# Bias of v folded into the projection bias: its columns written by GpSimd at attention's beginning, the product copied by ScalarE and added by GpSimd

## The chip, the cores and the metric

The kernel runs on one core of one Trainium2 chip, as one program in one launch. The metric is the device time of one execution in microseconds (us). Three timed runs of the kernel before gave 1572.09, 1574.92 and 1575.85 us; the median is 1574.92 us.

The engines are named as the profile names them: PE (TensorE matmul), PEld (TensorE weight load), DVE (VectorE), ACT (ScalarE), POOL (GpSimd) and SP (SyncE, which here only issues DMAs). Each runs its own queue in order and waits on semaphores.

## The reference

One transformer block with binarized attention weights and a ternary MLP, in float32. `x` is 4 x 1024 x 256, there are 16 heads of 16 columns.

```python
x = x + layernorm(attention(layernorm(x)))
x = x + layernorm(mlp(layernorm(x)))

def binlinear(x, W, b):                 # alpha: one number per row of W
    return x @ (alpha(W) * sign(W)).T + b
# attention
q, k, v = (split_heads(binlinear(x, W, b)) for W, b in ((Wq, bq), (Wk, bk), (Wv, bv)))
y = softmax(q @ k.T * scale) @ v
return binlinear(merge_heads(y), Wp, bp)
# mlp: tlin(x, w, s) = (x @ w.T) * s, w in {-1, 0, 1}
h = silu(tlin(x, w1, s1)) * tlin(x, w2, s2)
h = gelu(tlin(h, h1, sh1)); h = gelu(tlin(h, h2, sh2))
return tlin(h, w3, s3)
```

Rows of the softmax sum to one, so `bv` passes through attention unchanged. The kernel therefore leaves `bv` out of v and adds `(bv @ sign(Wp).T) * alpha_p` to `bp` once. Only that small piece is changed here: a 256-vector, held as the same row on all 128 partitions.

## The kernel before, in words

**Stages.** A short opening loads x and the weights, takes their signs and magnitudes, and normalises the first half of batch 0. `attention(True)` follows, a schedule that is written out by hand: the order in the source is the order in each engine's queue. Then the MLP runs over eight blocks of 512 tokens.

**Attention.** A block is 512 queries of one batch and four heads; there are 32. Each is worked in eight steps. A step has a first pass (L717: scores with queries on partitions, then a maximum on DVE, L726) for the block that comes next, and a second pass (L763: scores with keys on partitions, minus the maximum; the exponential on ACT, L773) with the product with v (L789) for the current block. Steps -10 to -1 hold only first passes of block 0 and 1 and the work that has to be done once: the projections of q, k and v of batch 0 (L561 for the first four heads, L530 for the others, L489 for v), the alphas (`alphas`, L992 and L999), and `projection_bias` at step -2. At the beginning of step -2 the maxima of block 0 are combined (`combine`: L733 on DVE, L735 to L737 on POOL), and in step -1 they are turned by PE (`shift`, L743) and copied by ACT (L750, `nmT`). The second pass of block 0 starts at step 0 with that copy.

**PSUM banks.** `through` is seven banks of 128 x 512. `bank()` gives out the bank that a small cost model (`clock`, `free_at`) holds to be free first; `put` and `got` keep that model and state the dependences, so the choice of the bank, made when the program is built, decides which reader a matmul waits for.

**The piece in question.** `projection_bias` first makes `bv_cols` on DVE (L396: each value of `bv` repeated along a row of 128), PE multiplies it with the signs of `Wp` (L401, two matmuls over one bank), DVE multiplies the bank by `az_bc`, the alphas of `Wp` (L406), and DVE adds that to `bz_bc` (L407). `bz_bc` is read for the first time when the first half of batch 0 is projected (L647), long after. `bv_cols` is a tile of the tag `full`, which has two buffers and also carries the pieces of q and k on their way from ACT (L537) to POOL (L543, L544). From those, SP copies the heads of the second four into place with 24 DMAs (L600).

**GpSimd's beginning.** On entering attention POOL clears `negmax` (L347), sets the ones in v's tiles (L431, L432) and clears `yn` (L436) and `bits` (L898), while DVE normalises the second half of batch 0 (L460, `xn`) and PE and ACT make the first heads' q (L561, L567). Later POOL also gathers the low bits of the MLP's weights (`gather`, L921 to L924) through a tile `half` of 128 x 512.

Of the kernel before, what the change touches and what calls it, by code (L numbers as in the profile page):

```python
# [30 lines left out]
F32 = mybir.dt.float32  # L31
# [4 lines left out]
ALU = mybir.AluOpType  # L36
# [4 lines left out]
P = 128  # L41
# [5 lines left out]
def sandwich_kernel(  # L47
# [24 lines left out]
    nc = tc.nc  # L72
    B, T, C = x.shape
    F = w1T.shape[1]
    KC = C // P
# [24 lines left out]
    ident = const.tile([P, P], F32, tag="ident", name="ident")  # L100
# [22 lines left out]
    bz_bc = const.tile([P, C], F32, tag="bz", name="bz_bc")  # L123
    az_bc = const.tile([P, C], F32, tag="az", name="az_bc")
# [16 lines left out]
    bv_sb = small.tile([P, KC], F32, tag="bv", name="bv_sb", bufs=1)  # L141
# [148 lines left out]
    def attention(signs):  # L290


        with ExitStack() as actx:
            ac = actx.enter_context(tc.tile_pool(name="ac", bufs=1))
# [5 lines left out]
            through = ps.tile([P, 7, 512], F32, tag="through", name="through")  # L300
# [4 lines left out]
            def bank():  # L305
                b = min(free_at, key=free_at.get)
                clock["PE"] = max(clock["PE"], free_at.pop(b))
                return b

            def state(access, engine, after, others, operands=()):  # L310
                for other in others:
                    tc.declare_no_dep(
                        access.ins, group=other, keep=[*after, *operands], reason="another bank"
                    )
                for earlier in after:
                    tc.add_manual_dep(access.ins, earlier.name, SYNC, reason="the same bank")
                tc.add_to_no_dep_group(engine, access.ins)
                return access.ins

            def put(b, access, operands=()):  # L320


                state(access, "PE", read[b], ("ACT", "DVE"), operands)
                if read[b]:
                    written[b].clear()
                    read[b] = []
                written[b].append(access.ins)
                clock["PE"] += 115

            def got(banks, engine, access, for_pe=False):  # L330

                others = [o for o in ("PE", "ACT", "DVE") if o != engine and not (for_pe and o == "PE")]
                after = [i for b in banks for i in written[b] + read[b]]
                lasts = {"ACT": 500, "DVE": 580}[engine]
                clock[engine] = max(clock["PE"] + 240, clock[engine] + lasts)
                for b in banks:
                    read[b].append(access.ins)
                    free_at[b] = clock[engine] + lasts + 150  # L340
                return state(access, engine, after, others)
# [7 lines left out]
            a2 = actx.enter_context(tc.tile_pool(name="a2", bufs=2))  # L349
# [23 lines left out]
            if signs:  # L373
                w_in = sign_of

                low = ac.tile([P, KC, T], F32R, tag="xnT", name="xnT_low")
                xnT_of = [[xnT_sb, low if b > 0 else w1_sb] for b in range(B)]
            else:
                w_in = {n: ac.tile([P, KC, C], F32, tag=f"w{n}", name=f"w{n}") for n in "qkv"}
# [10 lines left out]
                nc.vector.memset(alpha_sb, 1.0)  # L390
                nc.vector.memset(alpha_sb[:, 0, :], SCALE)

            def projection_bias():

                bv_cols = a2.tile([P, 2, KC, P], F32, tag="full", name="bv_cols")
                nc.vector.tensor_copy(  # L396
                    bv_cols[:, 0], bv_sb.unsqueeze(2).to_broadcast([P, KC, P])
                )
                t = bank()
                for i in range(KC):  # L400
                    put(t, nc.tensor.matmul(  # L401
                        through[:, t, :C], bv_cols[:, 0, i, :], w_in["p"].bitcast(F32)[:, i, :],
                        start=(i == 0), stop=(i == KC - 1),
                    ))
                product = bv_cols[:, 1].rearrange("p k o -> p (k o)")
                got([t], "DVE", nc.vector.tensor_mul(product, through[:, t, :C], az_bc))  # L406
                nc.vector.tensor_add(bz_bc, bz_bc, product)  # L407

            def load_scales():
                for dst, src in ((s1_sb, s1), (s2_sb, s2), (sh1_sb, sh1), (sh2_sb, sh2)):  # L410
# [486 lines left out]
            bits = ac.tile([P, 512], F32, tag="bits", name="bits")  # L897
            nc.gpsimd.memset(bits, 0)  # L898

            def weight_jobs():  # L900
                loads, stay, pass_by = [], [], []
                for dst, src in ((w1_sb, w1T), (h1a_sb, h1T[0 : F // 2, :]), (w2_sb, w2T)):
                    sv = src.rearrange("(k p) o -> p k o", p=P)
                    for k in range(0, sv.shape[1], 2):
                        loads.append(
                            lambda to=dst[:, k : k + 2, :], frm=sv[:, k : k + 2, :]:
                            nc.gpsimd.dma_start(to, frm)
                        )
                    for k in range(sv.shape[1]):
                        stay += [dst[:, k, bass.ts(j, 512)] for j in range(F // 512)]  # L910
                for src in (h1T[F // 2 : F, :], h2T, w3T):
                    sv = src.rearrange("(k p) o -> p k o", p=P)
                    width = min(512, sv.shape[2])
                    n = 512 // width
                    for k in range(0, sv.shape[1], n):
                        pass_by += [
                            sv[:, k : k + n, bass.ts(j, width)] for j in range(sv.shape[2] // width)
                        ]

                def gather(w):  # L920
                    low = w.bitcast(U16).rearrange("p (c half) -> p c half", half=2)[:, :, 0]  # L921
                    half = ac.tile([P, 512], F32, tag="half", name="half")
                    nc.gpsimd.tensor_copy(half, low)
                    nc.gpsimd.tensor_add(bits, bits, half)  # L924

                def load(i):
                    if i < len(pass_by):
                        raw_of[i] = a2.tile([P, 512], F32, tag="wraw", name=f"wraw_{i}")
                        nc.sync.dma_start(
                            raw_of[i].rearrange("p (k o) -> p k o", o=pass_by[i].shape[2]), pass_by[i]  # L930
                        )

                def take(i):
                    gather(raw_of.pop(i))
                    load(i + 2)

                some = small.tile([P, 1], F32, tag="some", name="some", bufs=1)

                def any_bits():

                    nc.vector.tensor_reduce(some, bits, AX.X, ALU.max)
                    nc.vector.tensor_scalar(some, some, 0.0, None, ALU.is_gt)

                def decide():

                    t = bank()
                    fl = through[0:1, t, 0:1]
                    put(t, nc.tensor.matmul(fl, some, row_ones, start=True, stop=True))
                    got([t], "DVE", nc.vector.tensor_copy(flag_sb, fl))

                *stay, last = [[lambda w=w: gather(w) for w in stay[i : i + 4]]
                               for i in range(0, len(stay), 4)]
                passing = [lambda i=i: take(i) for i in range(len(pass_by))]
                return loads, sum(stay, []) + [lambda: (load(0), load(1))] + passing, (
                    last + [any_bits, decide]
                )
# [76 lines left out]
            for m in range(NT // 2):  # L1033
                place((after + m, 0), lambda m=m: value(m))
            place((first + 8, 0), projection_bias)
            place((4, 0), load_scales)

# [389 lines left out]
    with tc.If(large < 1) as small_ones:  # L1427
        attention(True)
        few = nc.values_load(flag_sb)
        with tc.If(few < 1) as every_one:  # L1430
            mlp("", False, wp_sb)
        with every_one.Else():
            mlp("L", True, wp_sb)
    with small_ones.Else():
        attention(False)
        mlp("G", True, wp_all)
# [46 lines left out]
```

## Time and profile before

The profiled execution has a span of 1570.2 us; its own time is 1571.97 us, so 1.77 us lie around the span. It is 2.95 us below the median of the timed runs.

| view of the profile | what | us |
|---|---|---|
| busy over the span | PE 97%, DVE 68%, ACT 53%, POOL 28% | 1570.2 |
| timeline | opening, up to the first matmul of attention (L561) | 16.99 |
| timeline | first passes alone, up to the first L763 | 57.55 |
| chain of waits | attention's last product with v ends, the MLP's first matmul starts | 906.16 |
| groups | L726 DVE maximum of 128x512 | 0.680 each |
| groups | L646 and L647 POOL, two inputs, 128x256 | 0.733 and 0.736 each |
| tile `bv_cols` | DVE copy L396, multiply L406, add L407 | 0.294, 0.425, 0.425 |

A row of the timeline gives start and duration, engine, line, operation and output<-input; in brackets stands how long the engine sat idle before and what released it. A row of the chain of waits is a piece of work that the end depended on, in order of time. A row of the table by stretches gives, for each engine, its busy time in the stretch and in brackets the number of instructions (PE, PEld, DVE, ACT, POOL), then the clock that TensorE was granted as a share of full speed, the busy share of the DMA engines and GB/s.

### The profile page before, as it was taken

The numbers are of one execution on the slowest core, as the hardware profiler recorded it, in microseconds if no ns is written. First come the engines' busy times: TensorE is split into PE (matmuls) and PEld (weight loads), VectorE is DVE, ScalarE is ACT, GpSimd is POOL, SyncE is SP. The second block draws the span as 40 slices with busy tenths as digits, with TensorE's granted clock in tenths as the row PEclk, the third lists the DMA queues.
The fourth block names the chain that finished last, engine by engine and source line by source line (L and its number), as shares of the span: only waits on it lengthen the run. The fifth ranks groups of instructions, "written<-read, shape, count | busy, mean of one in ns | idle before, by whom it ended". The sixth has DMA issues, their size and how long they took to land.

```text
span 1570.2 us, 31816 instructions
## 1 busy us (share of the span) xinstructions
PE 1530.7 (97%) x12988; PEld 980.1 (62%) x12988; DVE 1075.3 (68%) x1960; ACT 829.2 (53%) x1495; POOL 437.6 (28%) x592
## 2 busy tenths in 40 slices
PE   7999999999999999999999999999999999999997
PEld 5544445444444444444444477888888888888886
DVE  7779887889887898878899554554545445444443
ACT  4477777777776777777777841413232313232321
POOL 2123133565333662414612150120202020202011
PEclk9799999999999999999999999999999999999999
DMA  1311521132133033211312040000000000000000
GB/s 58 72 19 34 152 47 22 30 75 60 47 79 61 13 70 76 61 29 35 76 36 71 8 138 0 1 14 1 14 1 14 1 14 1 14 1 14 1 14 16
DMA packets 35084, 58.55 MB, mean 37 GB/s; under 512 B 9968, under 2 KB 21488, under 8 KB 34928
## 3 DMA queue, kind: packets, MB, share of 16 engines
q1 hardware_dynamic: 29904, 43.70, 13.0%
q0 software_dynamic: 3792, 11.54, 2.4%
q8 instruction: 104, 1.70, 0.4%
q10 hardware_dynamic: 1232, 1.18, 0.2%
q14 instruction: 52, 0.43, 0.1%
HBM read 24.40 MB, written 4.19 MB: 18 GB/s over the span
## 4 chain that ended last, share of the span: by engine, by line
PE 83%; DVE 9%; ACT 4%; SPq 1%; issue 1%; POOL 1%; DMA 1%; POOLq 0%; DVEq 0%; ACTq 0%
PE g L1214 30%; PE y L789 14%; PE through L763 12%; PE through L717 9%; PE p L1214 7%; DVE nm L726 5%; PE fzp L1328 4%; PE through L530 2%; ACT e L773 2%; SPq L600 1%; PE through L743 1%; PE through L489 1%; PE through L632 1%; ACT ys L804 1%; DVE yt L830 1%
## 5 line engine op out<-in xcount | busy, mean ns | idle before, releaser
L726 DVE TENSOR_REDUCE nm<-through 128x1 f32<-128x512 f32 x1024 | 643.2, 680 | 113.7 <-PE through L717 58.0
L773 ACT ACTIVATE e<-through 128x512 f32<-128x512 f32 x1024 | 545.5, 603 | 161.9 <-PE through L763 145.6
L717 PE MATMUL through<-ks,qs 32*128 32x512 f32 x2048 | 462.5, 446 | 3.7 <-DVE nm L726 1.8
L763 PE MATMUL through<-qs,ks 32*128 32x512 f32 x2048 | 442.8, 435 | 11.2 <-ACT e L773 7.3
L763 PE MATMUL through<-nmT,ones_r 32*128 32x512 f32 x1024 | 349.3, 451 | 0.4 <-ACT nmT L750 0.4
L789 PE MATMUL y<-e,v 128*32 128x256 f32 x4096 | 322.2, 392 | 0.0
L717 PEld LDWEIGHTS through<-ks,qs 32*128 32x128 f32 x2048 | 216.0, 185 | 106.7 <-issue 83.8
L1214 PE MATMUL g<-g,h_sb 128*128 128x512 f32 x1024 | 235.7, 390 | 0.0
L763 PEld LDWEIGHTS through<-qs,ks 32*128 32x128 f32 x2048 | 202.6, 184 | 44.5 <-ACT e L773 20.8
L1214 PEld LDWEIGHTS g<-g,h_sb 128*128 128x128 f32 x1024 | 191.7, 188 | 39.5
L763 PEld LDWEIGHTS through<-nmT,ones_r 32*128 32x128 f32 x1024 | 137.9, 183 | 91.4 <-issue 88.3
L789 PEld LDWEIGHTS y<-e,v 128*32 128x32 f32 x4096 | 86.3, 108 | 170.8 <-issue 150.8
L1257 ACT ACTIVATE g2f<-g,sh_sb 128x512 f32<-128x512 f32 x64 | 44.1, 689 | 200.4 <-PE g L1214 177.4
L1257 ACT ACTIVATE g1f<-g,sh_sb 128x512 f32<-128x512 f32 x64 | 44.1, 690 | 169.7 <-PE g L1214 169.7
L164 POOL TENSOR_SCALAR ve_fz<-mvp_fz 128x4 f32<-128x4 f32 (+1 forms) x8 | 1.9, 234 | 470.7 <-DVE mvp_fz L176 470.7
L1214 PE MATMUL g<-h,h1b_sb 128*128 128x512 f32 x512 | 126.4, 389 | 0.0
L1214 PE MATMUL g<-h,h1a_sb 128*128 128x512 f32 x512 | 126.4, 389 | 0.0
L1184 DVE CAST g<-g2f 128x512 fp32r<-128x512 f32 x64 | 27.8, 434 | 142.0 <-ACT g2f L1257 142.0
L1214 PE MATMUL p<-xnT_sb,w_sb 128*128 128x512 f32 x512 | 117.7, 390 | 0.0
L1214 PEld LDWEIGHTS g<-h,h1b_sb 128*128 128x128 f32 x512 | 96.1, 188 | 19.9
L1214 PEld LDWEIGHTS g<-h,h1a_sb 128*128 128x128 f32 x512 | 96.1, 188 | 19.9
L1214 PEld LDWEIGHTS p<-xnT_sb,w_sb 128*128 128x128 f32 x512 | 95.6, 188 | 19.9 <-issue 0.4
(197 smaller groups left out, 1512.8 us busy)
## 6 DMA issues: line engine op xcount, KB each, us to landing
qs<-h1b_sb SPq DMA_DIRECT2D x240, 64.0 KB, 2.4
ks<-h1b_sb SPq DMA_DIRECT2D x120, 64.0 KB, 2.4
wraw<-in_dram SPq DMA_DIRECT2D x28, 256.0 KB, 2.7
h_sb<-in_dram POOLq DMA_DIRECT2D x4, 1024.0 KB, 8.2
yT<-yt SPq DMA_DIRECT2D x112, 32.0 KB, 2.0
out_dram<-x_sb SPq DMA_DIRECT2D x7, 512.0 KB, 2.8
x_sb<-in_dram SPq DMA_DIRECT2D x3, 1024.0 KB, 6.3
w_sb<-in_dram POOLq DMA_DIRECT2D x3, 1024.0 KB, 8.9
```

The costliest lines, as they stand in the source:

```text
L489: put(t, nc.tensor.matmul(through[:, t, bass.ts(i, C)], xnT_of[b][j][:, k, bass.ts(2 * m + i, P)], w_in["v"][:, k, :], start=(k == 0 and j ...
L530: put(t, nc.tensor.matmul(through[:, t, :], w_in[tag][:, k, bass.ts(c, P)], xnT_of[b][i][:, k, bass.ts(j, 512)], start=(k == 0 and i == 0) ...
L600: queue.dma_start(dst[to, :].bitcast(F32), src[rows, :].bitcast(F32))
L717: put(t, nc.tensor.matmul(through[:, t, :], q_of[u][n][rows, bass.ts(qt, P)], k_of[u][rows, bass.ts(j, 512)], start=(n == 0), stop=(n == 1),))
L726: got([t], "DVE", nc.vector.tensor_reduce(nm_of[blk][:, n4, j, g : g + 1], through[:, t, :], AX.X, ALU.max, negate=True))
L763: t, nc.tensor.matmul(through[:, t, :], lhs, rhs, start=(n == 0), stop=(n == 2)),
L773: exps.append(got([t], "ACT", nc.scalar.activation(e_of[s, g], through[:, t, :], AF.Exp)))
L789: nc.tensor.matmul(y_of[blk][32 * g : 32 * g + 32, cols], v_sb[n // 2][:, n % 2, :, :].rearrange("p h d -> p (h d)")[:, bass.ds((4 * g4 + ...
L1184: nc.vector.tensor_copy(hi, full)
L1214: nc.tensor.matmul(out[c], wk, src[j][:, k, :], start=(k == 0 and i == 0 and j == 0), stop=(k == n_k - 1 and i == len(ws) - 1 and j == 1),)
L1257: nc.scalar.activation(g, ps, AF.Gelu, scale=scale[:, c : c + 1])
L1328: nc.tensor.matmul(out_ps[i][:, :C], g2[j][:, k, bass.ts(i, P)], wk, start=(k == 0 and n == 0 and j == 0), stop=(k == NF - 1 and n == len( ...
```

## The change

The columns of `bv` are made once at the beginning of attention, on POOL instead of DVE, into a tile `spare` that stays: for each of the two columns, `ident * 0 + bv` over 128 x 128. In `projection_bias` the DVE copy is gone, ACT copies the product out of PSUM, and POOL multiplies it by `az_bc` and adds it to `bz_bc`. `gather` uses `spare` in place of `half`, which no longer exists; `bv_cols` no longer takes a turn in the tag `full`. The bank's reader is now stated to be ACT, so the cost model gives out the next banks in another order.

```diff
+            spare = ac.tile([P, 512], F32, tag="spare", name="spare")
+            bv_cols = spare[:, 0:C].rearrange("p (k o) -> p k o", k=KC)
+            for i in range(KC):
+                nc.gpsimd.tensor_scalar(
+                    bv_cols[:, i, :], ident, 0.0, bv_sb[:, i : i + 1], ALU.mult, ALU.add
+                )
+
             def projection_bias():
 
-                bv_cols = a2.tile([P, 2, KC, P], F32, tag="full", name="bv_cols")
-                nc.vector.tensor_copy(
-                    bv_cols[:, 0], bv_sb.unsqueeze(2).to_broadcast([P, KC, P])
-                )
                 t = bank()
                 for i in range(KC):
                     put(t, nc.tensor.matmul(
-                        through[:, t, :C], bv_cols[:, 0, i, :], w_in["p"].bitcast(F32)[:, i, :],
+                        through[:, t, :C], bv_cols[:, i, :], w_in["p"].bitcast(F32)[:, i, :],
                         start=(i == 0), stop=(i == KC - 1),
                     ))
-                product = bv_cols[:, 1].rearrange("p k o -> p (k o)")
-                got([t], "DVE", nc.vector.tensor_mul(product, through[:, t, :C], az_bc))
-                nc.vector.tensor_add(bz_bc, bz_bc, product)
+                product = spare[:, C : 2 * C]
+                got([t], "ACT", nc.scalar.copy(product, through[:, t, :C]))
+                nc.gpsimd.tensor_mul(product, product, az_bc)
+                nc.gpsimd.tensor_add(bz_bc, bz_bc, product)
...
                 def gather(w):
                     low = w.bitcast(U16).rearrange("p (c half) -> p c half", half=2)[:, :, 0]
-                    half = ac.tile([P, 512], F32, tag="half", name="half")
-                    nc.gpsimd.tensor_copy(half, low)
-                    nc.gpsimd.tensor_add(bits, bits, half)
+                    nc.gpsimd.tensor_copy(spare, low)
+                    nc.gpsimd.tensor_add(bits, bits, spare)
```

## The prediction, as put on record before the change was run

> **What bounds the kernel now.** I read the page first, then the chain of waits around the change, then the waits of that stretch, the table by stretches for the clock, and last the timeline of the opening, where two instructions are added.
>
> ```profile
> PE 1530.7 (97%) x12988; PEld 980.1 (62%) x12988; DVE 1075.3 (68%) x1960; ACT 829.2 (53%) x1495; POOL 437.6 (28%) x592
> PEclk9799999999999999999999999999999999999999
> ```
>
> PE carries the whole span, so only a place where PE stands still or runs slowly can give time back. The clock row has its one dent after the first slice in the second, 39 to 79 us, and `projection_bias` lies there. The chain of waits:
>
> ```profile
> 46.21 2.48 DVE nm L726 x4
> ...
> 48.72 0.06 DVE nmfull L733
> 48.79 0.04 issue
> 48.83 0.30 DVE bv_cols L396
> ...
> 49.18 2.07 PE through L401 x4
> 51.25 1.15 PE through L717 x4
> 52.40 2.00 PE through L530 x4
> 54.40 1.15 PE through L717 x3
> 55.55 1.05 PE through L743 x4
> ```
>
> The chain leaves PE at 46.21: DVE first works off four maxima, then the combination, then makes the columns, and only then can L401 start. The waits say the same:
>
> ```profile
> PE through L401 <- DVE bv_cols L396: 2.5, 1, 2.5
> ACT full_False L537 <- PE through L530: 10.4, 2, 8.6
> ```
>
> ACT meanwhile idles for up to 8.6 us. What follows the stall runs at half clock:
>
> ```profile
> 45.00:48.50 3.50, 1.70 (x11) 0.70 (x9) 3.21 (x6) 0.37 (x1) 1.70 (x2) 1.00 0.00 0
> 48.50:55.40 6.90, 6.22 (x16) 3.32 (x16) 2.97 (x8) 0.78 (x1) 0.64 (x4) 0.50 0.00 0
> 55.40:58.80 3.40, 3.40 (x22) 2.46 (x22) 2.07 (x4) 0.59 (x1) 1.84 (x2) 0.50 0.34 60
> 58.80:62.20 3.40, 3.27 (x29) 2.05 (x26) 3.40 (x7) 2.88 (x6) 0.00 (x0) 1.00 0.44 77
> 62.20:69.00 6.80, 6.80 (x53) 3.01 (x53) 4.07 (x7) 3.14 (x6) 0.00 (x0) 0.50 0.59 103
> ```
>
> The clock is 1.00 in the stretch with the stall, 0.50 for 10.2 us after it, 1.00 again, then 0.50 a second time. In rows of 1 us its steps lie at about 48.5, 58.8, 62.2 and 69.0, always about 3.4 us apart or a multiple of it, as if it were set anew every 3.4 us by the stretch before. From 69 us to the MLP it stays at 1.00.
>
> **The change part by part.** Times count from the span's start of the execution of before.
>
> *The stall.* The columns are ready at about 19 us, so L401 waits for nothing on DVE but its bank, whose last maximum ended at 44.7. PE's L717 group in front starts at 45.44; such a group at 40.27 takes 0.68, here its last pair also waits for ACT's az_bc, done at 45.92. I let L401 start at 46.5 instead of 49.18: -2.7.
>
> *The clock behind it.* With no gap I expect 1.00 to hold up to the end of L743. At full clock the same work costs: L401 1.06 (L999, same form, four records in 1.06 on the chain), L717 0.66 (43.79), L530 1.12 (42.66), L717 0.66, L743 0.57 (at 81.41: 0.65 with its tail), together 4.07, so L743 ends at 50.57. Before it took 49.18 to 56.60, 7.42. That is -3.35. Ends: 0 if the clock falls all the same, -3.35 if it holds; I take the latter, since 38.3 to 41.7, with the same sort of work, held 1.00.
>
> The Trainium skill (TensorE: Matmul & The Clock Gate, Part 1: The HAM clock gate) says that the half clock comes after at least one idle window of about 3.4 us, free-running. By that rule a gap of 2.5 us need not have cost the clock and the sum would hold the 2.7 alone; the row 49 to 58 at 0.50 disagrees, so I go by the row.
>
> *What PE meets on the way.* The order of the built program shows the same sequence on PE, with five PSUM groups that follow another reader and from there on the same pattern in other banks. Group by group: L717 behind L401 reuses its bank and waits for ACT's new copy, 47.56 + 0.1 + 0.37 (L1003, same form) = 48.03, while PE comes there at 48.2; L530 and the next L717 wait for maxima that ended at 46.8 and 47.4; L743 waits for POOL's negmax, 49.63, and PE comes at 50.0. Nothing binds, but cover is 0.2 to 0.4 us. Three more semaphore waits in front of L401: under 0.1.
>
> *DVE.* L396, L406, L407 (0.29 + 0.42 + 0.42) and the 2.16 between them go. The next maximum starts at about 48.85 instead of 52.44; the four of block 1 that were done when the second pass began are done by 51.3 again. No further gain, it is the same chain.
>
> *ACT's copy*, 0.37, falls into its idle 8.6: 0. Behind it stands full_False at 49.4.
>
> *POOL's product and sum*, 0.73 + 0.74 (L646, L647) = 1.47, stand behind negmax (49.63) and ahead of the last piece of k (L543, L544), which was ready at 50.2 and now starts at 51.1. SP's 24 DMAs of heads wait for it: first issue at 51.75 instead of 56.00, last one 14.2 later at 66.0 instead of 70.18, landed (0.6 to issue, 2.3 in flight) at 68.9. Their first readers, first passes of the second four heads, stand six steps after the second pass starts: 77.0 before, 71.0 now. Cover falls from 3.9 to 2.1 us; 0, and beyond 8 us of gain the DMAs would be what is late next. SP's queue behind them (x of batch 1, the scales) moves up too.
>
> *The second stretch at half clock.* Steps 0 and 1 have no product with v; DVE works its maxima without a break there, and 3.4 us of it dropped the clock. That stays, shifted along: 0. Ends: -3.0 if it does not come (57.4 to 69.86 is 12.5; 2.4 steps of 2.5 and 3.3 make 9.3), +1.7 if one more 3.4 us falls to half.
>
> *The columns on POOL.* Two instructions of 128 x 128, each between 0.24 (L200 copies, start to start) and 0.61 (half of L460 on POOL, 128x256, 1.22), on an engine that then idles 15 us. What they can hurt is DVE beside them:
>
> ```profile
> 17.08 0.53 POOL L347 MEMSET negmax<- 128x512 f32 x1
> 17.25 2.89 DVE L460 TENSOR_SCALAR xn<-x_sb,mvp_x,rsp_x 128x256 f32<-128x256 f32 x4 [0.40 <-POOL rsp_x L166]
> 18.50 0.53 POOL L898 MEMSET bits<- 128x512 f32 x1
> 19.20 0.78 ACT L567 ACTIVATE qs<-through,bias,alpha 128x512 fp32r<-128x512 f32 x1 [2.88 <-DVE xn L460]
> ```
>
> The first of the four takes 1.92, the others 0.40: it comes through only as POOL's memsets end. Ends: +1.2, if it now also waits for both columns, and 0. I take 0, by the nearest rows with a POOL that reads: at 983.8 and 984.6 a DVE scale took 0.83 instead of 0.41, so it waited for one POOL addition and went ahead of the next; at 10.59 four xn ran at 0.40 beside POOL copies. An xn that comes earlier gains nothing: PE gives ACT the next bank only at 20.7. `spare` for `half` in 44 gathers: the same two POOL instructions, 0.
>
> **Sum:** -2.7 - 3.35 = -6.0, so 1571.97 becomes 1566.0. The median of the runs is 2.95 above that execution: 1574.92 - 6.0 = 1568.9. PE is busy or held by its own pace from there to the end, so I let the gain reach the end whole. What this kernel's times can tell from no change is about 0.3%, 4.7 us.
>
> **The rivals.**
>
> *xn held by the columns* (0.18). The chain from 17.25 on runs through xn, ACT and L561 at 24.47, so +1.15 there is +1.15 at the end: 1570.1. If PE's gap before 24.5 costs another 3.4 us at half clock, +1.7 more: 1571.8. For it: all of POOL's eleven instructions in a row went ahead of xn. Against: those were memsets, the columns read.
> The Trainium skill (SBUF — State Buffer, Who interferes with whom) states this as a rule: POOL and a DVE instruction in a two-port mode lock each other out for a whole instruction, by order of issue. The 1.92 agrees; whether the lock passes over between two reading POOL instructions is what differs.
>
> *The clock falls anyway* (0.12). The new stretch still has many matmuls over 32 rows. Then the stall alone: 1574.92 - 2.7 = 1572.2.
>
> *The second half-clock stretch goes too* (0.06): up to 3.0 more, limited by the DMAs above to about 2.1: 1566.8.
>
> *Slower* (0.07). One mechanism: xn held at the opening, with PE losing 3.4 us stretches at half clock for it (1.7 each). At 1.22 per column, the whole of L460's row, +2.45 and two stretches make +5.85, which only cancels the gain: 1574.8. It decides from a delay of 2.6 us with two stretches on; slower by 0.3% needs over 7 us and two. Nothing in the profile shows such a hold; the chance is for what I don't see.
>
> **How the numbers follow.** The forecast has 0.57 and a range of its own from 1567 to 1570.5, by the spread of the runs shown (1.9) and where the 3.4 us happen to fall. Faster by over 0.3% (below 1570.2): 0.9 of it, the case with more gain, and 0.45 of the held xn: 0.51 + 0.06 + 0.08 and a little of the clock case = 0.66. Slower by 0.3%: 0.05 of the last rival's 0.07. The rest, 0.29, is within. The range reaches from the case with more gain less the spread, 1565.2, to the clock case plus some of it, 1573.0.
>
> **What would show it.** Right: no wait of PE above 0.3 us in front of L401 or the group behind it; L401's records at 0.3 us instead of 0.63; clock 1.00 from 28 us to at least 52; L743 near 50.6 and the first L763 near 51.4 instead of 57.55; xn's first instruction at most 1.9 us. Wrong: xn above 2.5 us; clock 0.50 at 49 to 52; PE waiting for ACT's new copy, or first passes of the second four heads waiting for DMAs near 71 us.

## The result, and the profile after

The changed kernel takes 1566.16 us (median of 6 runs, 1562.58 to 1568.80), against 1574.93 us for the kernel before beside it (6 runs, 1572.09 to 1576.95). The ratio is 0.9945, with a 95% interval of 0.993 to 0.9959. The forecast was 1568.9 us, with a range from 1565.2 to 1573.0 and 0.66 for faster by over 0.3%.

The profiled execution has a span of 1561.5 us and took 1563.28 us. Two rows of its page, busy time and the granted clock:

```profile
PE 1524.4 (98%) x12988; PEld 977.1 (63%) x12988; DVE 1074.3 (69%) x1957; ACT 829.6 (53%) x1496; POOL 439.5 (28%) x596
PEclk9999999999999999999999999999999999999999
```

The dent of the second slice is gone. The chain of waits through the same place:

```profile
45.49 1.19 PE through L722 x8
46.68 1.06 PE through L405 x4
47.74 0.95 PE through L722 x5
48.69 1.12 PE through L535 x4
49.81 0.66 PE through L722 x3
50.47 0.59 PE through L748 x4
51.06 0.71 PE through L722 x5
51.77 4.28 DVE nm L731 x7
```

The chain now stays on PE. DVE's four maxima, the combination and the columns no longer stand in it; the bias matmuls (L405, before L401) start at 46.68 instead of 49.18 and take 1.06 instead of 2.07. The turning of the maxima (L748, before L743) ends at 51.06 instead of 56.60. In the waits of this stretch the new parts on ACT and POOL stand in two rows:

```profile
PEld through L748 <- POOL spare L411: 0.4, 1, 0.4
PEld through L722 <- ACT spare L410: 0.2, 1, 0.2
```

PE no longer waits ahead of L405. The first row is no new cost: where POOL has no such instruction (e_cols below), the same weight load waits the same 0.4 us behind POOL's `negmax`. The one new hold on PE's path is the second row: the scores behind the bias reuse its bank and wait 0.2 us for ACT's copy, so that group takes 0.95 us instead of 0.66. The table by stretches, for the clock (the number behind the five engines' busy times):

```profile
45.00:48.50 3.50, 3.50 (x20) 1.84 (x18) 3.20 (x6) 0.74 (x2) 1.68 (x2) 1.00 0.00 0
48.50:55.40 6.90, 6.79 (x50) 3.94 (x49) 6.47 (x13) 3.54 (x6) 3.84 (x7) 1.00 0.13 23
62.20:69.00 6.80, 6.80 (x96) 3.16 (x92) 6.02 (x11) 4.88 (x10) 0.00 (x0) 1.00 0.48 83
```

Both stretches that ran at 0.50 before now run at 1.00: the one behind the stall, which the forecast counted on, and the second one at 62 us, which it took as staying. The second one is why this execution gains more than forecast. The MLP's first matmul starts at 897.22 instead of 906.09, 8.87 us earlier, and the span is 8.7 us shorter. In the opening, the columns:

```profile
17.63 0.53 POOL L347 MEMSET negmax<- 128x512 f32 x1
17.80 3.00 DVE L465 TENSOR_SCALAR xn<-x_sb,mvp_x,rsp_x 128x256 f32<-128x256 f32 x4 [0.41 <-POOL rsp_x L166]
18.15 0.77 POOL L397 TENSOR_SCALAR spare<-ident,bv_sb 128x128 f32<-128x128 f32 x2
19.74 0.78 ACT L572 ACTIVATE qs<-through,bias,alpha 128x512 fp32r<-128x512 f32 x1 [2.88 <-PE through L566]
```

The four `xn` take 3.00 us in all, against 2.89 before. The first two run beside the columns (0.385 each) and take 0.51 and 0.46 us; it is now the third, from 18.61 us on, that takes 1.87.

Does the larger gain belong to the change, or to where this execution's half-clock stretches fell? The runs below are read with one table. It cuts each profiled execution at three points that the chain and the timeline give: attention's first matmul, the bias matmuls' start, the end of the turning of the maxima, and the MLP's first matmul. The last column lists the half-clock stretches, in units of 3.4 us, with their start.

| execution | opening to bias, us | bias to end of turning | from there to the MLP | at half clock |
|---|---|---|---|---|
| before | 32.19 | 7.42 | 849.5 | 24.7 (1), 48.6 (3), 62.2 (2) |
| after | 29.14 | 4.38 | 846.2 | 26.2 (1) |
| after_again | 33.39 | 4.38 | 846.3 | 30.3 (3) |
| after_third | 33.62 | 4.39 | 849.0 | 25.9 (4), 60.0 (2) |
| e_cols | 29.30 | 4.10 | 849.4 | 25.5 (1), 56.2 (2) |
| e_product | 35.94 | 7.08 | 849.5 | 29.8 (3), 53.7 (5) |
| e_fill_before | 35.70 | 4.17 | 848.5 | 30.5 (3) |
| e_cols_act | 33.40 | 4.39 | 849.2 | 30.1 (3), 518 (1), 737 (1) |
| e_pool_late | 33.39 | 4.38 | 849.3 | 30.0 (3), 518 (1), 737 (1) |
| e_fill_steps | 33.36 | 4.39 | 850.6 | 30.1 (3) |
| e_fill_open | 29.15 | 4.39 | 849.3 | 513 (1), 732 (1) |
| e_fill_open_again | 29.17 | 4.39 | 848.1 | 513 (1) |
| e_fill_open_last | 37.91 | 4.37 | 848.8 | 24.1 (6), 522 (1) |

### The profile page after: what moved, and what is told of

Read it like the earlier page. It is cut to its first block, busy times and chain, and to the rows that moved or that the text cites. A ratio compares the mean times of both kernels' runs of the same rounds, so it can differ in the third digit from the quotient of the medians.

```text
span 1561.5 us, 31820 instructions
## 1 busy us (share of the span) xinstructions
PE 1524.4 (98%) x12988; PEld 977.1 (63%) x12988; DVE 1074.3 (69%) x1957; ACT 829.6 (53%) x1496; POOL 439.5 (28%) x596
## 4 chain that ended last, share of the span: by engine, by line
PE 84%; DVE 9%; ACT 4%; issue 1%; POOL 1%; DMA 0%; SPq 0%; DVEq 0%; ACTq 0%; POOLq 0%
PE g L1218 30%; PE y L794 14%; PE through L768 12%; PE through L722 10%; PE p L1218 7%; DVE nm L731 6%; PE fzp L1332 4%; PE through L535 2%; ACT e L778 2%; PE through L494 1%; PE through L748 1%; PE through L637 1%; ACT ys L809 1%; DVE bnstp_x L175 1%; DVE yt L835 1%
## 5 line engine op out<-in xcount | busy, mean ns | idle before, releaser
L768 PE MATMUL through<-qs,ks 32*128 32x512 f32 x2048 | 441.8, 433 | 11.3 <-ACT e L778 7.3
L768 PE MATMUL through<-nmT,ones_r 32*128 32x512 f32 x1024 | 348.2, 449 | 0.4 <-ACT nmT L755 0.4
L768 PEld LDWEIGHTS through<-qs,ks 32*128 32x128 f32 x2048 | 201.4, 183 | 45.0 <-ACT e L778 20.5
L768 PEld LDWEIGHTS through<-nmT,ones_r 32*128 32x128 f32 x1024 | 137.3, 182 | 90.9 <-issue 87.9
```

The source lines that it names most:

```text
L768: t, nc.tensor.matmul(through[:, t, :], lhs, rhs, start=(n == 0), stop=(n == 2)),
```

## Experiments

**The changed kernel again.** The kernel is unchanged; it ran twice more, each time beside other variants.

> The changed kernel once more, unaltered, for a second profiled execution and more times. Theory (the extra 2.7 us beyond the forecast are the second half-clock stretch, which comes in some executions and not in others): 1562 to 1569 us, with the granted clock of an execution falling as its time rises, and this profile either like the first (no half clock after 30 us) or some 3 us longer with half clock somewhere between 52 and 66 us. Rival (the second stretch is gone for good and the scatter has another source): no half clock after 30 us in any profile, and time and clock not tied together.

> The changed kernel again, beside the one with the filled opening on the same chip. Median 1566 to 1568 us, and in the profiled execution a half-clock stretch of one or three quanta of 3.4 us that begins between 26 and 31 us.

The first gave 1567.54 us (12 runs, 1563.12 to 1571.43; ratio 0.996, 0.9946 to 0.9974), the second 1567.50 us (5 runs, 1564.70 to 1569.95; ratio 0.9954, 0.994 to 0.9967). The table by stretches of the first one:

```profile
26.80:30.20 3.40, 2.54 (x10) 1.42 (x11) 2.48 (x5) 2.41 (x4) 0.00 (x0) 1.00 0.00 0
30.20:40.50 10.30, 10.30 (x42) 7.05 (x42) 6.57 (x12) 1.95 (x3) 1.88 (x2) 0.51 0.01 2
```

and of the second:

```profile
26.00:39.60 13.60, 13.60 (x52) 8.25 (x45) 7.62 (x13) 4.82 (x7) 1.89 (x2) 0.50 0.00 1
60.20:66.90 6.70, 6.70 (x53) 2.87 (x53) 3.95 (x7) 3.07 (x6) 0.00 (x0) 0.50 0.60 105
```

One program ran in three ways. In the first profile after, the opening lost one unit of 3.4 us, here three and four; the bias matmuls then start 33.4 to 33.6 us behind attention's first matmul instead of 29.1. In the last execution the stretch of steps 0 and 1, as in the kernel before, is back, and the way from there to the MLP is 849.0 instead of 846.2 us: it costs 2.8. So the second stretch was not taken away for good; it comes in some executions. Neither opening is as expected: three units from 30.3 us and four from 25.9. That the granted clock of an execution falls as its time rises held: from 0.997 at 1563 us to 0.990 at 1571. What is the same in all three is the middle column: 4.38 or 4.39 us, and no wait ahead of the bias.

Over all executions the kernel after has a mean of 1567.05 us (23) and the kernel before 1573.60 (94). The difference is 6.55 us, 5.4 to 7.7 by resampling these executions.

**The product back on DVE.** Only the columns are made early; ACT's copy and POOL's two instructions are undone.

```diff
-                got([t], "ACT", nc.scalar.copy(product, through[:, t, :C]))
-                nc.gpsimd.tensor_mul(product, product, az_bc)
-                nc.gpsimd.tensor_add(bz_bc, bz_bc, product)
+                got([t], "DVE", nc.vector.tensor_mul(product, through[:, t, :C], az_bc))
+                nc.vector.tensor_add(bz_bc, bz_bc, product)
```

> One part alone: the columns made by GpSimd at the beginning, the product multiplied and added by DVE as before. Theory (L401 was held because its columns stood in DVE's queue; who reads the product matters little): PE reaches the bias matmul at about 46.5 us without a wait, the clock stays at 1.00; DVE's two instructions of 0.42 come in after the combination and put the next maximum at 49.7 instead of 48.8, so at most 0.9 us worse than the full change: 1566 to 1568. Rival (DVE's load was the matter): half of the gain or less, 1570 to 1575.

1567.57 us (12 runs, 1563.74 to 1576.18), ratio 0.9971 (0.9953 to 0.9988); the mean is 1568.86. In the chain of waits DVE's two instructions stand ahead of the maxima that the second pass needs:

```profile
48.84 0.44 DVE spare L410
...
49.30 0.43 DVE bz_bc L411
49.73 6.59 DVE nm L730 x11
```

The next maximum starts at 49.73, against 48.79 after: 0.94 us, the two instructions' own 0.87 and the gap between them. The mean is 1.8 us above after, but with an interval from -0.6 to 4.4. The trace shows the delay of 0.9 us; the times alone can't tell it from zero. The clock stayed at 1.00 through the bias, as expected, and fell only at 56.2 us. Most of the gain is here already.

**The columns back at the old place.** Only the product moves to ACT and POOL; DVE makes the columns in `projection_bias`.

```diff
-            for i in range(KC):
-                nc.gpsimd.tensor_scalar(
-                    bv_cols[:, i, :], ident, 0.0, bv_sb[:, i : i + 1], ALU.mult, ALU.add
-                )
...
             def projection_bias():
 
+                nc.vector.tensor_copy(bv_cols, bv_sb.unsqueeze(2).to_broadcast([P, KC, P]))
                 t = bank()
```

> The other part alone: the columns made by DVE at the old place, the product copied by ACT and finished by GpSimd. Theory: the wait of 2.5 us before the bias matmul and the half clock behind it stay, and with them the time: 1573 to 1575. Rival (DVE's load): half of the gain or more, below 1571.

1575.76 us (12 runs, 1570.83 to 1579.21), ratio 1.0011 (0.9996 to 1.0026): no gain at all, and a little above what was expected. Its chain is that of before:

```profile
50.20 2.48 DVE nm L728 x4
...
52.70 0.04 DVE nmfull L735
...
52.88 0.31 DVE spare L399
...
53.23 1.63 PE through L402 x4
...
59.27 1.05 PE through L745 x4
```

The table by stretches shows PE's gap and what follows it:

```profile
50.20:53.50 3.30, 0.75 (x3) 0.31 (x3) 2.94 (x6) 0.00 (x0) 1.03 (x4) 1.00 0.00 0
53.60:70.60 17.00, 17.00 (x92) 10.36 (x90) 10.22 (x16) 7.17 (x13) 3.40 (x5) 0.50 0.31 55
```

PE again waits 2.5 us for the columns, and the clock goes to half behind it, at 53.7 us and for five units. Against after_again, whose opening also lost three units, the wait adds 2.55 us (35.94 against 33.39) and the slow work 2.70 (7.08 against 4.38). The early columns carry the gain, the product's move by itself nothing that can be measured.

**Wait kept, gap filled.** The kernel before, with five matmuls that nobody reads (the next matmul overwrites the bank) while PE waits for the columns. It parts the clock from the wait.

```diff
                 t = bank()
+                at = clock["PE"]
+                for i in range(5):
+                    put(t, nc.tensor.matmul(
+                        through[:, t, :C], avg, mag_of["p"][:, i % KC, :], start=True, stop=True
+                    ))
+                clock["PE"] = at
```

> The kernel before with five extra matmuls of 128x256 (of the averaging matrix with the magnitudes, overwritten by the bias matmul) in front of the bias matmul, to keep PE busy during its wait without shortening it. Theory (the stall costs twice, 2.7 us of waiting and 3.4 us of half clock after it): the bias matmul still starts at about 49.2 us, the clock stays at 1.00 behind it, L743 ends near 53.3 us instead of 56.6, and the time is 1574.9 - 3.4 = 1571.5, or up to 3 less if the second half-clock stretch goes as well. Rival (the clock falls for the thin matmuls behind the wait, not for the wait): no change, 1574 to 1576.

1571.81 us (12 runs, 1569.55 to 1573.97), ratio 0.9989 (0.9979 to 0.9999). The chain, and two rows of the table by stretches:

```profile
52.46 0.30 DVE bv_cols L396
...
52.81 1.13 PE through L407 x4
53.94 0.66 PE through L723 x5
54.60 1.13 PE through L536 x4
55.73 0.66 PE through L723 x2
56.39 0.59 PE through L749 x4
```

```profile
52.00:54.00 2.00, 1.88 (x11) 1.07 (x11) 0.74 (x4) 0.00 (x0) 0.60 (x3) 1.00 0.00 0
54.00:75.00 21.00, 20.79 (x223) 10.78 (x224) 19.18 (x32) 13.63 (x26) 1.89 (x2) 1.00 0.43 75
```

The wait is still there (35.70 us to the bias, 2.31 more than after_again), but the clock stays at 1.00 behind it, and the work there takes 4.17 us instead of 7.42 in before and 7.08 in e_product. So 2.9 to 3.25 us belong to the gap's effect on the clock, apart from the wait. The whole gains less than that; PE meets new waits later, of which the largest is

```profile
PE through L723 <- DVE mvp_x L176: 1.1, 1, 1.1
```

It lies at 564.8 us, and one of 1.0 us at 782.6; together they are about the 2.2 us by which the third column exceeds after_again. Why they come is not shown: the edit sets the cost model's `clock` back, so by the source the order of the banks is that of before.

**Columns on ACT.** The rival in the forecast was that `xn` is held by POOL's columns. Here ACT, idle at that time, makes them.

```diff
-                nc.gpsimd.tensor_scalar(
-                    bv_cols[:, i, :], ident, 0.0, bv_sb[:, i : i + 1], ALU.mult, ALU.add
-                )
+                nc.scalar.activation(
+                    bv_cols[:, i, :], ident, AF.Identity, scale=0.0, bias=bv_sb[:, i : i + 1]
+                )
```

> The full change, but the two columns are made by ACT at attention's beginning, so GpSimd's row of instructions is as long as in the kernel before. Theory (the columns on GpSimd cost nothing, because the first xn goes ahead and PE sets the pace there): xn's first instruction again takes 1.9 us, the matmuls behind it come no earlier, 1566.2 give or take 1. Rival (the columns hold DVE's xn and that is paid): 0.7 us or more better.

1566.37 us (8 runs, 1563.15 to 1570.59), ratio 0.9952 (0.9934 to 0.9969), the same as after. The row of `xn` (duration min/median/max, first and last start):

```profile
L465 DVE TENSOR_SCALAR xn<-x_sb,mvp_x,rsp_x x4: 396/402/1923, 17.7 to 20.2; 128x256 f32<-128x256 f32 x4
```

After has in this row:

```profile
L465 DVE TENSOR_SCALAR xn<-x_sb,mvp_x,rsp_x x4: 398/483/1873, 17.8 to 20.4; 128x256 f32<-128x256 f32 x4
```

With no columns on POOL the first `xn` takes 1.92 us; with them the first two go through and the third takes 1.87. Either way the held one ends 0.14 or 0.15 us behind POOL's last memset (19.62 and 19.48 us here, 20.48 and 20.33 in after). So it is POOL's memsets that hold `xn`, and the columns cost 0.11 us of the four together. From `xn`'s start to the first scores it is 6.02 us here and 6.01 after.

**POOL 2.9 us later.** Four more multiplications behind the sum (their result is not used) test the cover that the forecast gave to the 24 DMAs of heads.

```diff
                 nc.gpsimd.tensor_add(bz_bc, bz_bc, product)
+                for _ in range(4):
+                    nc.gpsimd.tensor_mul(product, product, az_bc)
```

> The full change with four more GpSimd multiplications of 0.73 us behind the addition (their result is not used), so the last piece of k and the 24 DMAs of the second four heads come 2.9 us later. Theory (in the changed kernel these DMAs have no cover left: the last one was issued at 67.7 us, lands near 70.6, and its readers stand at 68.4 to 70.1): PE waits there and 2 to 3 us are lost, 1568 to 1569.5. Rival (the forecast's cover of 2.1 us is still there): at most 0.8 us lost, 1566 to 1567.

1567.26 us (12 runs, 1563.02 to 1571.60), ratio 0.9959 (0.9944 to 0.9975). The first DMA of k's heads is issued at 58.95 instead of 55.76 (after_again), the last at 72.75 instead of 71.14, and PE waits for none of them. The 3 us that this execution lies above after_again in the third column are the two single units at half clock, at 518 and 737 us; e_cols_act has the same two and the same 849.2 us without the extra work on POOL. So PE waited for none of these DMAs, and the theory that their cover was used up fell.

**Filling steps 0 and 1.** Four extra matmuls of 128x256 (their output is read by nobody) in four slots of the two steps without a product with v, to keep the second stretch at full clock.

```diff
+                    if signs and s in (0, 1) and i in (1, 3):
+                        fill()
                     for step, part in parts:
                         attend(step, part)
```

> The full change with two extra matmuls of 128x256 in each of steps 0 and 1 (into y's bank, before y is begun), where DVE sets the pace and PE's work is thin. Theory (in some executions those two steps drop the clock for some 3 to 7 us): no half clock after 30 us in any execution, the median falls to 1563 to 1564.5 and the scatter shrinks. Rival (the scatter has another source, or the extra matmuls cost as much as they keep): 1566 or more, scatter as before.

1572.66 us (12 runs, 1569.19 to 1579.27), ratio 1.0 (0.9986 to 1.0014), 8 to 9 us above what was expected. The chain shows why:

```profile
55.83 0.73 PE through L768 x5
56.57 0.63 PE y_fill L1076 x2
57.20 0.43 PE through L768 x3
```

The fillers lie in the chain itself. From the turning to the MLP it takes 850.6 us instead of 846.3, although no stretch there runs at half clock. PE has gaps in these steps, but its queue is in order, and the scores behind each filler are what ACT and DVE wait for. The theory that there is slack to fill in these steps fell.

**Filling the opening.** The opening's half clock came three or four units long in most of the profiles so far. Ten 128x128 matmuls that nobody reads go into the three places ahead of it where PE stands idle.

```diff
+                def fill(times):
+                    for _ in range(times):
+                        nc.tensor.matmul(
+                            y_fill[:, :P], ident, ident, start=True, stop=True,
+                            skip_group_check=True,
+                        )
+
+                fill(4)
+                place((first, 1), lambda: fill(2))
                 place((first, 1), lambda: first_heads(False, 1))
...
+                    if signs and (s, i) == (first + 2, 1):
+                        fill(4)
```

> The changed kernel with ten more small matmuls (the identity by itself, 128x128, their output read by nobody) put into the three places ahead of 30 us where TensorE stands idle in every trace so far: four behind the transposes that end at 22.8 us (idle to 23.7), two ahead of the projection at 24.9 us (idle from 24.4), four ahead of the scores at 29.1 us (idle from 28.3). Theory: these idle stretches let the half-clock stretch begin at 30.2 us in most executions and last three quanta of 3.4 us, which cost 4.2 us (bias matmuls at 50.7 instead of 46.6 us). Then the clock stays whole through 30 to 40 us, the bias matmuls start at 46.6 to 47 us, and the median falls from 1567 to about 1563. Rival: the stretch is owed to something else (the slow operands' reads, the idle time ahead of 17.5 us, or the chip's power), and comes anyway: bias matmuls at 50.7 us, median 1567 to 1568, the fillers adding 0 to 0.3 us.

> The kernel with all three idle places of the opening filled, once more. Theory (the idle places bring the opening's half clock on): no half clock before 50 us whatever the grid's position, bias matmuls 29.2 us behind the first matmul of attention, all executions within 2 us of one another, median 1563 to 1565 us, and 2 to 4 us less than the changed kernel beside it. Rival (the first profile was one lucky position of the 3.4 us grid): half clock of 3.4 or 10.2 us comes in the opening again, median within 1 us of the changed kernel's.

> Of the ten small matmuls only the last four, in the idle place from 28.3 to 29.1 us; the places at 22.8 and 24.4 us stay idle. If the idle 0.86 us just before the stretch decides, it stays away as with all three filled: median 1563.5 to 1565 us. If all idle time of the opening counts, the stretch comes with one or three quanta: median 1566 to 1568 us.

All three places: 1564.27 us (6 runs, 1563.29 to 1565.45; ratio 0.9939, 0.9923 to 0.9955), then 1563.36 us (5 runs, 1563.08 to 1568.10; ratio 0.9941, 0.9925 to 0.9956). Only the last four: 1570.34 us (12 runs, 1564.71 to 1576.04; ratio 0.9981, 0.9966 to 0.9996). The table by stretches of e_fill_open:

```profile
26.80:30.20 3.40, 3.40 (x21) 2.41 (x19) 3.19 (x6) 1.73 (x3) 0.00 (x0) 1.00 0.00 0
30.20:40.50 10.30, 10.30 (x71) 6.65 (x69) 9.36 (x16) 3.91 (x6) 3.77 (x4) 1.00 0.01 2
513.30:516.70 3.40, 3.40 (x30) 1.29 (x32) 2.36 (x5) 1.94 (x4) 0.70 (x1) 0.50 0.20 73
```

and of e_fill_open_last:

```profile
24.10:44.50 20.40, 20.10 (x70) 13.22 (x71) 10.64 (x18) 5.05 (x7) 1.89 (x2) 0.50 0.00 1
```

With all three places filled, PE is busy all through 26.8 to 30.2 us (2.54 of 3.40 in after_again), the opening stays at 1.00 in both profiles from 22 us on, and the bias comes 29.15 and 29.17 us behind attention's first matmul. With the last place alone, six units run at half clock from 24.1 on and the bias comes after 37.91 us: the gaps at 22 and 24 us are still open, and the fillers then take 2.08 us instead of 1.16. Its median lies above both expected ranges. So an early gap can bring the half clock by itself, and filling the last place does not help then. That the last gap does no harm is not shown: in after_again the stretch before the half clock, 26.8 to 30.2, holds that gap, and no run filled the early two alone. The mean over both runs with all three places filled is 1564.32 us (11 executions) against 1567.05 for after: 2.7 us better, 1.4 to 4.0 by resampling; against before it is 9.3 us. On the chip that ran both, the medians were 1563.36 and 1567.50. One of the eleven still took 1568.10 at a mean clock of 0.994, against the expected 2 us between all executions; it has no profile. This version beats both kernels.

## Why the prediction was right

*The stall, -2.7.* Right. The bias starts at 46.68 by the chain, forecast 46.5. Counted from attention's first matmul, before and after, with one unit lost in each opening, differ by 3.05 us (32.19 against 29.14). Between executions whose openings lost three units the wait is worth 2.55 us (e_product against after_again).

*The clock behind it, -3.35.* Right in mechanism and nearly in size: 7.42 became 4.38, not the forecast 4.07, so -3.04 instead of -3.35. The part that was priced too low is the group behind the bias: 0.95 instead of 0.66, since PE came to the reused bank before ACT's copy (0.37 us, from 47.77 on) had ended; the cover of 0.2 to 0.4 us did not hold. In e_cols, where DVE reads that bank, the same work takes 4.10. e_fill_before shows that this part is the clock and not the wait: filling a gap of 2.5 us kept the clock whole. In after_again it fell at 30.3 us behind a window in which PE was busy 2.54 us of 3.40. The Trainium skill (TensorE: Matmul & The Clock Gate, Part 1: The HAM clock gate) lets the clock fall after at least one idle window of about 3.4 us. These runs differ from it, since none of the windows was idle throughout. The same section of the Trainium skill says that the windows run free and that one kernel differs from run to run by their position. The three profiles of one program, with half clock from 26.2, 30.3 and 25.9 us, agree.

*What was to be seen.* The second pass's first scores (L768) start at 51.74, forecast 51.4; the bias matmuls last 0.38 us each, before 0.63, forecast 0.3; PE's wait behind the bias is 0.2, below the 0.3 named. The clock at 1.00 from 28 us on was wrong: the opening's half clock lasted to 29.6 us in the first profile and to 40.5 and 39.6 in the other two. It is found in the kernels with the old columns too (three units in e_product and e_fill_before), so it is no part of the gain.

*The columns on POOL, 0.* Right, and for the reason given: beside the columns the first two `xn` take 0.51 and 0.46 us, and the one that is held, now the third, comes through as POOL's memsets end. The rival "xn held by the columns" (0.18) fell.

*POOL's product and the DMAs, 0.* Right. The first DMA of k's heads is issued at 51.66, forecast 51.75; the last at 67.71 instead of 66.0; e_pool_late delays them further at no cost that shows. The limit that the forecast saw at 8 us of gain did not bind: after gained 8.9, and PE waited for no DMA there.

*DVE's 0.42 + 0.42, in the chain.* Right: the next maximum starts at 48.79, forecast 48.85, and with the two instructions back on DVE 0.94 us later.

*The second stretch, 0.* Wrong for the profiled execution after, where it did not come and 3.3 us more were gained (849.5 against 846.2), and right for after_third, where it came. As a term it is a chance, not a yes or no, and the rival with its 1566.8 us (0.06) was given too little. That its time lies near the median is in part luck: it held the gain to 2.1 us for the sake of the DMAs, and after gained 3.3. Of the nine profiles with early columns and nothing added in steps 0 and 1, two have the stretch (after_third, e_cols). Of the three with the old columns before has it, e_product's half clock behind the wait runs on over it, and e_fill_before has none.

*The sum, -6.0.* The two parts that belong to the change, 2.55 to 3.05 and 3.04, make 5.6 to 6.1 us; the mean gain over all executions is 6.55 (5.4 to 7.7). Between the two profiles the parts add up: attention's first matmul comes 0.55 us later in after (17.54 against 16.99; after_third has 17.04, so this is not the change), the stall gives 3.05, the clock behind it 3.04, the second stretch 3.3, together 8.84 of the 8.87 us at the MLP's first matmul. What this execution gained beyond the forecast is thus the second stretch, the term put at nothing. The median of 1566.16 lies 2.7 us below the forecast, those of the two repeats 1.4. Whether the second stretch is rarer with early columns can't be said from so few profiles.

## What to carry to other kernels

A short wait of PE is priced by what it does to the clock behind it as much as by its own length: here 2.5 us of wait cost 5.6 to 6.1. Filler matmuls repair that where PE truly waits for another engine (the opening, -2.7 us), and cost where PE's queue feeds the engines that set the pace (+4 us in steps 0 and 1). Where the half clock falls differently from one execution to the next, cut the traces at fixed points and compare each part with an execution whose opening is alike, before a difference of some microseconds is put down to an edit.

## What the hardware showed unexpectedly

The opening of one and the same program ran at half clock for 3.4, 10.2 or 13.7 us, which moves the bias by up to 4.5 us and with it the end. With the opening's gaps filled ten of eleven executions lay between 1563.1 and 1565.5 us; without, 23 lay between 1562.6 and 1571.4.

Single units of half clock also came in the middle of attention, in five profiles from 513 to 522 us and in three of these again from 732 to 737. Against after_again, which has none, the third column is longer by 1.5 to 2.5 us for each of them (849.3, 848.1 and 848.8 with two, one and one).

Why one given window costs the clock and a similar one does not stays open. In before, the window from 58.8 to 62.2 us had PE busy for 3.27 us of 3.40 by its record and the next one ran at half clock, while in after 53.47 to 56.88 had 3.31 of 3.41 and none followed. PE's busy time alone does not decide it: in e_fill_before 20.24 to 23.65 had 1.70 us of 3.41 and the next one ran at full clock, and in after 22.75 to 26.16 had 2.06 and the next one ran at half.

The clock column of the table by stretches can't be trusted at the very beginning. In after the projection's matmuls (L566) stand 0.43 us apart from 18.1 to 20.7 us, where the column gives 1.00, and again from 27.9 to 28.7, where it gives 0.50; at 25.0 to 25.8 us and 1.00 they stand 0.23 apart.
